# The first layer of whole expert tiles, computed turned from a standing copy of its weights

## The chip, the cores and the metric

The kernel runs on one core of one Trainium2 chip. The metric is device time in microseconds (us). Names of the engines: PE is the matrix engine (PEld its weight loads), DVE the vector engine, ACT the scalar engine, POOL and SP the two that mostly issue transfers here.

## What is computed

A graph layer of 4096 nodes with 512 features: masked attention over an adjacency matrix, then a mixture of experts. The change touches only the experts:

```
logits = xf @ Wg + bg                       # 8 experts
topk_scores, topk_idx = top_k(logits, 2)
topk_w = softmax(topk_scores)
h = gelu(einsum('nd,edh->neh', xf, W1) + b1)      # erf form
y = einsum('neh,ehf->nef', h, W2) + b2
out = sum over the 2 chosen experts of topk_w * y ; x = x + out
```

D = HID = 512, E = 8, everything in float32.

## The kernel before

The stages before the experts project q, k and v and build lists of neighbours (to about 456 us in the profile), run attention over gathered rows (to about 1455 us) and route the nodes (to about 1508 us): each node's normalized row is scattered into a buffer `xs_d` sorted by expert. The weights W1 and W2 of all 8 experts stand in SBUF from then on, in eight parts `wparts[c]` (parts 0 to 3 are the four 128-row chunks of W1, 4 to 7 those of W2), in the freed `ring` and one tile `w`.

The expert stage works through 66 tiles of 128 rows in an order written out by hand (`tiles`, L1464). 57 of them (`b < FULL`) hold rows of one expert: whole tiles. 9 are mixed (`b >= FULL`): their two halves of 64 rows belong to two experts, and the second half's weights are fetched for the tile into `wo_` by `load_other` (L1369, 8 transfers, and a ninth for its bias row `bo`). Mixed tiles stand in the sequence at place 7 and then every sixth.

The parts of one tile, each a function:

- `fetch` (L1287): SP loads the tile's rows.
- `turn` (L1362, L1364): PE transposes the rows in four pieces of 128x128 into `pt_e`, ACT copies them out as `xT`.
- `hidden` (L1393): loads the tile's expert number into registers of PE and DVE (L1395), and multiplies: four accumulating matmuls into `ph`, with a piece of `xT` standing in the array and 512 columns of W1 moving. DVE copies the result to `h` (L1407).
- `turn_hidden` (L1410): PE transposes `h` in four pieces into `pht`; DVE adds the bias `b1T` while it takes them out as `hT` (L1419), ACT applies gelu (L1424).
- `second` (L1427): four matmuls with a piece of `hT` standing and W2 moving, into `py`; DVE computes the row weights (L1438, L1441, L1444) and adds the bias row from `bb` (L1449; for the two halves of a mixed tile L1451 and L1452), ACT scales (L1453), and POOL scatters the rows into the output with an adding transfer (L1458).

Tiles overlap: in the loop of `tiles`, step n issues `turn_hidden(b)`, `hidden(after)`, `turn(third)`, `second(b)`, where `after` and `third` are the next two tiles; before a mixed tile `turn(third)` comes ahead of `hidden(after)`. Every engine executes its instructions in the order issued. Ahead of the first tile come 60 transposes that keep PE busy (`warm`, L1357) and `halves` (L1303 to L1349), in which DVE works out the table of the mixed tiles' experts, with two small matmuls (L1336) in its middle. A pool's tile with `bufs=1` is one buffer, so that its next writer waits for its last reader.

Of the kernel before, what the change touches and what calls it, by code (L numbers as in the profile page):

```python
# [9 lines left out]
F32 = mybir.dt.float32  # L10
# [10 lines left out]
P = 128  # L21
# [54 lines left out]
def _fast(ctx, tc, dram, flag, x, adj, Wks, Wqs, Wvs, Wo, Wg, bg, W1, b1, W2, b2, out):  # L76
    nc = tc.nc
    N, D = x.shape
    H, _, KD = Wks.shape
    E, _, HID = W1.shape  # L80
    DC = D // P
    HC = HID // P
# [17 lines left out]
    FULL = -(-(2 * N - E * (P - 1)) // P)  # L100
    Q = P // 2
# [232 lines left out]
    with ExitStack() as s1:  # L334
# [213 lines left out]
        for h in range(NHC):  # L548
# [4 lines left out]
            g, c = divmod(h, NH)  # L553
# [91 lines left out]
    with ExitStack() as s2:  # L645
# [81 lines left out]
        def turn(s):  # L727
            st = steps[s]
            i = st["i"]
            nk = len(st["kv"])  # L730
            pk = bank(f"pkT_{s}", [2 * NP, P])
            for x, g in enumerate(st["kv"]):
                for p in range(NP):
                    nc.tensor.transpose(pk[:, x * NP + p, :], g[:, ts(p, P)], ident)  # L734
            kT = step.tile([P, 2 * NP, P], F32, tag="kT", name=f"kT_{s}")
            nc.scalar.copy(kT[:, : nk * NP], pk[:, : nk * NP])  # L736
            st["kT"] = [kT[:, x * NP : (x + 1) * NP] for x in range(nk)]
            t = step.tile([P, NW, 16], U16, tag="t", bufs=6, name=f"t_{s}")
            if st["kind"] == "own":
                words = [own_words[:, i, :]]  # L740
            else:
                words = [wv[:, i * NW : (i + 1) * NW] for wv in st["wv"]]
            nw = NW // len(words)
            for x, wv in enumerate(words):
                w = slice(x * nw, (x + 1) * nw)
                nc.vector.tensor_tensor(
                    t[:, w], wv[:, w].unsqueeze(2).to_broadcast([P, nw, 16]), bits[:, w],
                    op=ALU.bitwise_and,
                )
            st["t"] = t.rearrange("p w k -> p (w k)")  # L750
            if st["kind"] == "own":
                m = step.tile([P, P], F32, tag="m", bufs=2, name=f"m_{s}")
                nc.vector.scalar_tensor_tensor(
                    m, st["t"], 0.0, eye, op0=ALU.is_gt, op1=ALU.max
                )
                st["m"] = m
# [507 lines left out]
    with ExitStack() as s4:  # L1264
# [89 lines left out]
        def warm():  # L1354
            pt = ps_t.tile([P, HC, P], F32, tag="t", name="pt_warm")
            for k in range(60):
                nc.tensor.transpose(pt[:, k % HC, :], ident, ident)  # L1357
# [11 lines left out]
        def load_other(b):  # L1369

            n = 2 * (b - FULL) + 1
            e = nc.values_load(
                tableq[:, n : n + 1], engines=(SP, DVE), min_val=0, max_val=E - 1,
                skip_runtime_bounds_check_because=why,
            )
            wo_ = otherp.tile([P, DC + HC, 1, HID], F32, tag="w", name=f"wo_{b}")
            for c in range(DC + HC):
                from_, k = (W1, c) if c < DC else (W2, c - DC)
                nc.sync.dma_start(
                    out=wo_[:, c],  # L1380
                    in_=from_[bass.ds(e, 1), ts(k, P), :].rearrange("e p f -> p e f"),
                )
            bo = otherp.tile([P, D], F32, tag="b", name=f"bo_{b}")
            nc.sync.dma_start(out=bo, in_=b2[bass.ds(e, 1), :].partition_broadcast(P))
            other[b] = e, wo_, bo

        def sides(b, c):
            w = wparts[c][:, bass.ds(es[b], 1), :]
# [1 line left out]
                return [(slice(0, P), w)]  # L1390
            return [(slice(0, Q), w), (slice(Q, P), other[b][1][:, c])]

        def hidden(b):  # L1393
            at = table[:, b : b + 1] if b < FULL else tableq[:, 2 * (b - FULL) :][:, :1]
            es[b] = nc.values_load(  # L1395
                at, engines=(PE, DVE), min_val=0, max_val=E - 1,
                skip_runtime_bounds_check_because=why,
            )
            ph = ps_h.tile([P, HID], F32, tag="h", name=f"ph_{b}")
            for c in range(DC):  # L1400
                for a, w in sides(b, c):
                    nc.tensor.matmul(  # L1402
                        ph[a], xTs[b][:, c, a], w, start=(c == 0), stop=(c == DC - 1),
                        skip_group_check=b >= FULL,
                    )
            h = work.tile([P, HID], F32, tag="h", name=f"h_{b}")
            nc.vector.tensor_copy(h, ph)  # L1407
            hs[b] = h

        def turn_hidden(b):  # L1410
            pt = ps_t.tile([P, HC, P], F32, tag="t", name=f"pht_{b}")
            for c in range(HC):
                nc.tensor.transpose(pt[:, c, :], hs[b][:, ts(c, P)], ident)
            hT = work.tile([P, HC, P], F32, tag="hT", name=f"hT_{b}")
            whose = [(slice(0, P), es[b])]
            if b >= FULL:
                whose = [(slice(0, Q), es[b]), (slice(Q, P), other[b][0])]
            for a, e in whose:
                nc.vector.tensor_tensor(  # L1419
                    hT[:, :, a], pt[:, :, a],  # L1420
                    b1T[:, bass.ds(e, 1), :].rearrange("p e c -> p (e c)").unsqueeze(2)
                    .to_broadcast([P, HC, a.stop - a.start]), op=ALU.add,
                )
            nc.scalar.activation(hT, hT, AF.Gelu)  # L1424
            hTs[b] = hT

        def second(b):  # L1427
            py = ps_y.tile([P, D], F32, tag="y", name=f"py_e{b}")
            for c in range(HC):
                for a, w in sides(b, DC + c):  # L1430
                    nc.tensor.matmul(  # L1431
                        py[a], hTs[b][:, c, a], w, start=(c == 0), stop=(c == HC - 1),
                        skip_group_check=b >= FULL,
                    )
            r = rows[b]
            wt = work.tile([P, 1], F32, tag="wt", name=f"wt_{b}")
            rest = work.tile([P, 1], F32, tag="rest", name=f"rest_{b}")
            nc.vector.tensor_scalar(  # L1438
                rest, r[:, D + 3 : D + 4], -1.0, 1.0, op0=ALU.mult, op1=ALU.add
            )  # L1440
            nc.vector.tensor_scalar(  # L1441
                wt, r[:, D + 1 : D + 2], pos[:, b : b + 1], rest, op0=ALU.is_equal, op1=ALU.mult,
            )
            nc.vector.tensor_scalar(  # L1444
                wt, wt, r[:, D + 3 : D + 4], r[:, D + 2 : D + 3], op0=ALU.add, op1=ALU.mult
            )
            y = work.tile([P, D], F32, tag="y", bufs=3, name=f"y_{b}")
            if b < FULL:
                nc.vector.tensor_add(y, py, bb[:, bass.ds(es[b], 1), :])  # L1449
            else:  # L1450
                nc.vector.tensor_add(y[:Q], py[:Q], bb[:Q, bass.ds(es[b], 1), :])  # L1451
                nc.vector.tensor_add(y[Q:], py[Q:], other[b][2][Q:])  # L1452
            nc.scalar.mul(y, y, wt)  # L1453

            n = P if b < FULL else Q
            for k in range(0, P, n):
                whose = r[:n, D : D + 1] if k == 0 else tokens[b]
                nc.gpsimd.indirect_dma_start(  # L1458
                    out=out,
                    out_offset=bass.IndirectOffsetOnAxis(ap=whose.bitcast(I32), axis=0),  # L1460
                    in_=y[k : k + n], in_offset=None, compute_op=ALU.add,
                )

        def tiles(seq, first=False):  # L1464
            mixed = [b for b in seq if b >= FULL]
            for b in seq[:4]:
                fetch(b)
            if first:
                nc.sync.dma_start(
                    out=bb.rearrange("p e f -> p (e f)"),  # L1470
                    in_=b2.rearrange("e f -> (e f)").partition_broadcast(P),
                )
                warm()
                halves()
            load_other(mixed.pop(0))
            turn(seq[0])
            hidden(seq[0])
            if len(seq) > 1:
                turn(seq[1])
            for n, b in enumerate(seq):  # L1480
                after, third = (seq[n + 1 : n + 3] + [None, None])[:2]
                if n + 4 < len(seq):
                    fetch(seq[n + 4])
                turn_hidden(b)
                if third is not None and after >= FULL:
                    turn(third)
                if after is not None:
                    hidden(after)
                if third is not None and after < FULL:
                    turn(third)  # L1490
                second(b)
                if b >= FULL and mixed:
                    load_other(mixed.pop(0))
# [565 lines left out]
```

## Time and profile before

| | us |
|---|---|
| timed runs, median of 3 (lowest, highest) | 2287.24 (2279.12, 2288.51) |
| profiled execution, its own time | 2042.98 |
| its span, first to last instruction | 2041.2 |
| busy in the span: PE, PEld | 1926.3, 1275.3 |
| busy: DVE, ACT, POOL | 968.6, 791.2, 569.4 |
| the expert stage in it | about 1508 to 2024, and a tail to the end |

The profile comes from one profiled execution. A line of it names the line of the kernel, the engine, the operation, what it writes and reads (`out<-in`), a count, busy time and mean length in ns. A matmul's record is longer than the time after which the next can start, since matmuls are pipelined: distances between starts are what counts. One float32 matmul has two records, for two passes, each with its own weight load; a transpose has one. The mean granted clock of PE was 0.981 of full speed.

### The profile page before, as it was taken

The numbers are of one execution on the slowest core, as the hardware profiler recorded it, in microseconds if no ns is written. First come the engines' busy times: TensorE is split into PE (matmuls) and PEld (weight loads), VectorE is DVE, ScalarE is ACT, GpSimd is POOL, SyncE is SP. The second block draws the span as 40 slices with busy tenths as digits, with TensorE's granted clock in tenths as the row PEclk, the third lists the DMA queues.
The fourth block names the chain that finished last, engine by engine and source line by source line (L and its number), as shares of the span: only waits on it lengthen the run. The fifth ranks groups of instructions, "written<-read, shape, count | busy, mean of one in ns | idle before, by whom it ended". The sixth has DMA issues, their size and how long they took to land. (4 is left out here: it accounts for less than half of the span.)

```text
span 2041.2 us, 59938 instructions
## 1 busy us (share of the span) xinstructions
PE 1926.3 (94%) x25581; PEld 1275.3 (62%) x25581; DVE 968.6 (47%) x2519; ACT 791.2 (39%) x1166; POOL 569.4 (28%) x716
## 2 busy tenths in 40 slices
PE   8799999998999898998999998999889999999997
PEld 4344444448887787887878887777654444444443
DVE  4455556634544464564555554454543333333332
ACT  3233333315555554654545454545312222222221
POOL 2000000016333326345362635324121222222221
PEclk9899999999999999999999999989989999999998
DMA  9877877249688859779687786858874555555542
GB/s 369 272 262 258 259 264 261 83 170 384 224 272 272 276 191 375 252 247 352 236 296 279 265 304 241 309 187 322 285 261 93 127 117 114 112 117 119 114 68 44
DMA packets 193602, 462.00 MB, mean 226 GB/s; under 512 B 30384, under 2 KB 46768, under 8 KB 193200
## 3 DMA queue, kind: packets, MB, share of 16 engines
q0 software_dynamic: 66784, 248.65, 38.4%
q1 hardware_dynamic: 102096, 178.04, 26.8%
q10 hardware_dynamic: 24448, 31.38, 4.5%
q8 instruction: 206, 3.38, 0.7%
q14 instruction: 68, 0.56, 0.1%
HBM read 385.37 MB, written 72.64 MB: 224 GB/s over the span
## 5 line engine op out<-in xcount | busy, mean ns | idle before, releaser
L707 POOL DMA_INDIRECT ring<-kv_d,idx x361 | 358.7, 994 | 851.7 <-issue 471.6
L778 ACT ACTIVATE pr<-ps 128x1024 f32<-128x1024 f32 x270 | 270.0, 1025 | 370.8 <-PE ps L771 367.0
L784 DVE SCALAR_TENSOR_TENSOR pr<-t,pr 128x1024 f32<-128x1024 uint16 x238 | 284.0, 1222 | 236.7 <-ACT pr L778 236.2
L771 PE MATMUL ps<-q,kT 64*64 64x64 f32 (+1 forms) x10224 | 306.6, 237 | 29.1 <-issue 23.8
L799 PE MATMUL o<-ring,pr 128*64 128x65 f32 x8640 | 297.3, 226 | 26.1 <-issue 26.0
L771 PEld LDWEIGHTS ps<-q,kT 64*64 64x64 f32 (+1 forms) x10224 | 273.0, 148 | 71.3 <-issue 55.1
L799 PEld LDWEIGHTS o<-ring,pr 128*64 128x64 f32 x8640 | 274.3, 140 | 54.0 <-issue 51.4
L1402 PE MATMUL ph<-ring,xT 128*128 (+1 forms) x528 | 238.2, 594 | 0.8 <-ACT xT L1364 0.8
L734 PE MATMUL pkT<-ident,ring 128*128 128x128 f32 x1572 | 209.6, 283 | 10.2 <-DMA ring<-kv_d 5.9
L736 ACT COPY kT<-pkT 128x512 f32<-128x512 f32 (+1 forms) x270 | 198.9, 786 | 15.9 <-PE pkT L734 10.3
L1458 POOL DMA_INDIRECT out_dram<-y,r x66 | 102.0, 1545 | 367.7 <-ACT y L1453 238.9
L734 PEld LDWEIGHTS pkT<-ident,ring 128*128 128x128 f32 x1572 | 173.6, 143 | 28.7 <-issue 8.9
L1431 PE MATMUL py_e<-ring,hT 128*128 (+1 forms) x396 | 182.3, 596 | 1.6 <-ACT hT L1424 1.6
L1402 PEld LDWEIGHTS ph<-ring,xT 128*128 128x128 f32 (+1 forms) x528 | 91.3, 183 | 99.8 <-issue 98.7
L1453 ACT ACTIVATE y<-y,wt 128x512 f32<-128x512 f32 x66 | 47.6, 722 | 269.8 <-DVE y L1449 230.0
L615 PE MATMUL pv<-wv,xT 128*128 128x512 f32 x256 | 130.0, 603 | 0.0
L1407 DVE COPY h<-ph 128x512 f32<-128x512 f32 x66 | 45.6, 691 | 170.7 <-PE ph L1402 170.7
L615 PE MATMUL pk<-wk,xT 128*128 128x512 f32 x256 | 125.2, 608 | 0.7 <-ACT xT L409 0.7
L600 PE MATMUL pq<-xT,wq 128*128 128x512 f32 x256 | 123.1, 603 | 0.0
L844 PE MATMUL py<-wo,oT 128*128 128x512 f32 x256 | 119.1, 609 | 0.7 <-ACT oT L838 0.7
L1073 POOL DMA_INDIRECT xs_d<-x,slot_i x58 | 67.8, 1169 | 173.4 <-DVE x L1069 58.5
L1431 PEld LDWEIGHTS py_e<-ring,hT 128*128 128x128 f32 (+1 forms) x396 | 67.2, 183 | 75.9 <-issue 74.1
(281 smaller groups left out, 1900.2 us busy)
## 6 DMA issues: line engine op xcount, KB each, us to landing
adj<-in_adj_dram SPq DMA_DIRECT2D x64, 1024.0 KB, 5.6
wo<-in_L_ffn_W_dram SPq DMA_DIRECT2D x72, 256.0 KB, 4.9
kv_d<-kvr ACTq DMA_DIRECT2D x32, 516.0 KB, 4.4
ring<-kv_d SPq DMA_DIRECT2D x32, 516.0 KB, 7.0
r<-xs_d SPq DMA_DIRECT2D x57, 258.0 KB, 2.7
ring<-in_L_ffn_W_dram SPq DMA_DIRECT2D x56, 256.0 KB, 3.3
xt<-in_x_dram SPq DMA_DIRECT2D x32, 256.0 KB, 6.9
q_d<-qT ACTq DMA_DIRECT2D x32, 256.0 KB, 4.3
```

Of the source, the lines that this page charges most:

```text
L600: nc.tensor.matmul(pq, w["q"][:, c, ts(p, P)], xTs[b][:, c, :], start=(c == 0), stop=(c == DC - 1),)
L615: nc.tensor.matmul(pk, xTs[b][:, c, ts(t, P)], w[n][:, c, :], start=(c == 0), stop=(c == DC - 1),)
L707: nc.gpsimd.indirect_dma_start(out=g, out_offset=None, in_=kv_d, in_offset=bass.IndirectOffsetOnAxis(ap=idx[i // GL][:, i % GL, a : a + 1] ...
L734: nc.tensor.transpose(pk[:, x * NP + p, :], g[:, ts(p, P)], ident)
L736: nc.scalar.copy(kT[:, : nk * NP], pk[:, : nk * NP])
L771: nc.tensor.matmul(ps[c : c + nk, r, p * P + x * nq : p * P + (x + 1) * nq], kT[r * KD : (r + 1) * KD, p, c : c + nk], q[r * KD : (r + 1) ...
L778: nc.scalar.activation(pr.rearrange("p h q -> p (h q)"), ps.rearrange("p r f -> p (r f)"), AF.Exp)
L784: nc.vector.scalar_tensor_tensor(pr, st["t"].unsqueeze(1).to_broadcast([P, H, P]), 0.0, pr, op0=ALU.is_gt, op1=ALU.mult,)
L799: nc.tensor.matmul(o[c * HALF : (c + 1) * HALF, h // NP, (h % NP) * VW : (h % NP + 1) * VW], pr[:, hd * NP + p, c * HALF : (c + 1) * HALF] ...
L844: nc.tensor.matmul(hold["py"], hold["oT"][:, c, :], wo[:, c, :], start=(c == 0), stop=(c == NP - 1),)
L1402: nc.tensor.matmul(ph[a], xTs[b][:, c, a], w, start=(c == 0), stop=(c == DC - 1), skip_group_check=b >= FULL,)
L1431: nc.tensor.matmul(py[a], hTs[b][:, c, a], w, start=(c == 0), stop=(c == HC - 1), skip_group_check=b >= FULL,)
```

## The change

For whole tiles the roles in the first layer are exchanged. A new function `stand` loads the expert number and lets DVE copy the expert's W1 (four pieces of 128x512, `w1s`, a single buffer) to a fixed place. `hidden` then has 128x128 pieces of `w1s` standing in the array and `xT` moving, in 16 matmuls of 128 columns into the four quarters of `ph`. The result comes out with hidden features on the partitions, as `second` wants it, so that the bias and gelu (now `gelu_`) follow at once from `ph`; the copy to `h` and the four transposes are issued for mixed tiles alone. `stand` is issued a tile ahead: after `hidden(after)` for `third`, and for the first tile ahead of `halves`. The bias row `bo` of a mixed tile's second half is no more fetched; it is read from `bb`. `h` has one buffer in place of two.

```diff
-            bo = otherp.tile([P, D], F32, tag="b", name=f"bo_{b}")
-            nc.sync.dma_start(out=bo, in_=b2[bass.ds(e, 1), :].partition_broadcast(P))
-            other[b] = e, wo_, bo
+            other[b] = e, wo_
...
-        def hidden(b):
+        w1s = {}
+        def stand(b):
             at = table[:, b : b + 1] if b < FULL else tableq[:, 2 * (b - FULL) :][:, :1]
             es[b] = nc.values_load(
                 at, engines=(PE, DVE), min_val=0, max_val=E - 1,
                 skip_runtime_bounds_check_because=why,
             )
+            if b < FULL:
+                w1s[b] = work.tile([P, DC, HID], F32, tag="w1s", bufs=1, name=f"w1s_{b}")
+                for c in range(DC):
+                    nc.vector.tensor_copy(
+                        w1s[b][:, c], wparts[c][:, bass.ds(es[b], 1), :].rearrange("p e f -> p (e f)")
+                    )
+
+        def hidden(b):
             ph = ps_h.tile([P, HID], F32, tag="h", name=f"ph_{b}")
+            if b < FULL:
+                pt = ph.rearrange("p (c t) -> p c t", t=P)
+                for f in range(HC):
+                    for c in range(DC):
+                        nc.tensor.matmul(
+                            pt[:, f, :], w1s[b][:, c, ts(f, P)], xTs[b][:, c, :],
+                            start=(c == 0), stop=(c == DC - 1),
+                        )
+                gelu_(b, pt)
+                return
...
-            h = work.tile([P, HID], F32, tag="h", name=f"h_{b}")
+            h = work.tile([P, HID], F32, tag="h", bufs=1, name=f"h_{b}")
...
         def turn_hidden(b):
+            if b < FULL:
+                return
             pt = ps_t.tile([P, HC, P], F32, tag="t", name=f"pht_{b}")
             for c in range(HC):
                 nc.tensor.transpose(pt[:, c, :], hs[b][:, ts(c, P)], ident)
+            gelu_(b, pt)
+
+        def gelu_(b, pt):
             hT = work.tile([P, HC, P], F32, tag="hT", name=f"hT_{b}")
...
-                nc.vector.tensor_add(y[Q:], py[Q:], other[b][2][Q:])
+                nc.vector.tensor_add(y[Q:], py[Q:], bb[Q:, bass.ds(other[b][0], 1), :])
...
                 warm()
+                stand(seq[0])
                 halves()
+            else:
+                stand(seq[0])
             load_other(mixed.pop(0))
             turn(seq[0])
             hidden(seq[0])
             if len(seq) > 1:
                 turn(seq[1])
+                stand(seq[1])
...
                 if after is not None:
                     hidden(after)
+                if third is not None:
+                    stand(third)
                 if third is not None and after < FULL:
                     turn(third)
                 second(b)
```

## The prediction

> **What bounds the kernel now.** The share of busy time by stage comes first, since the change touches only the last stage; its columns are the stretch in us, its length, then busy us (and records) of PE, PE's weight loads (PEld), DVE, ACT and POOL, the granted clock, DMA share and GB/s.
>
> ```profile
> 1455.00:1508.00 53.00, 40.63 (x333) 33.64 (x331) 31.14 (x182) 8.00 (x15) 17.04 (x32) 0.82 0.86 302
> 1508.00:2024.00 516.00, 513.84 (x1717) 243.10 (x1718) 177.65 (x413) 120.39 (x197) 112.10 (x74) 1.00 0.51 110
> 2024.00:2042.00 18.00, 3.56 (x8) 1.29 (x8) 0.69 (x1) 0.72 (x1) 2.68 (x2) 0.69 0.24 34
> ```
>
> For 516 us of expert tiles PE is busy 513.84 at full clock; DVE is busy a third of the time. A busy PE need not be a dense one, so the timeline of one whole tile follows (start, length, operation, count).
>
> ```profile
> 1583.22 0.60 PE L1413 MATMUL pht<-ident,h 128*128 128x128 f32 x4
> 1583.66 3.60 PE L1402 MATMUL ph<-ring,xT 128*128 x8
> 1587.10 0.60 PE L1362 MATMUL pt_e<-ident,r 128*128 128x128 f32 x4
> 1587.53 2.74 PE L1431 MATMUL py_e<-ring,hT 128*128 x6
> 1590.11 1.02 PE L1431 MATMUL py_e<-w,hT 128*128 x2
> 1590.97 0.49 PE L1413 MATMUL pht<-ident,h 128*128 128x128 f32 x3
> ```
>
> Starts follow without a hole: 4 transposes of the hidden result 0.44 us, first layer 3.44, 4 transposes of the input 0.43, second layer 3.44; 7.75 us a tile. One f32 matmul is two passes (8 records for 4 matmuls) and a pass of 512 columns takes 3.44 / 8 = 0.43. So PE's order of work is the path, and what leaves PE leaves the time. The waits confirm it: in the stage DVE waits for PE (h for ph, y for py_e), and PE waits for others only in the first and last tile.
>
> ```profile
> DVE h L1407 <- PE ph L1402: 170.7, 66, 4.3
> ...
> DVE y L1449 <- PE py_e L1431: 137.3, 57, 3.7
> ...
> PE py_e L1431 <- ACT hT L1424: 1.6, 1, 1.6
> ...
> PE pht L1413 <- DVE h L1407: 0.4, 1, 0.4
> ```
>
> (Total us, times, longest.)
>
> **Part 1: transposes removed.** 57 whole tiles lose turn_hidden's four, 0.44 us each tile on PE's path: 57 x 0.436 (a transpose starts every 0.109) = -24.9 us.
>
> **Part 2: the first layer turned.** Per whole tile, 4 matmuls with 512 moving columns become 16 with 128, so 8 passes become 32, each with its own 128-column weight load. Moving columns stay 8 x 512 = 32 x 128, so 3.43 us if loads hide. But a load must now hide behind a quarter of the streaming. How fast can load and pass follow each other? The trace has no f32 pass of 128 columns over the full array, but three neighbours:
>
> ```profile
> 489.56 1.75 PEld L771 LDWEIGHTS ps<-q,kT 64*128 64x128 f32 x29 [0.93 <-issue]
> ...
> 1479.23 0.97 PEld L954 LDWEIGHTS pl<-wg,x2T 128*128 128x128 f32 x8 [0.79 <-ACT x2T L924]
> ```
>
> The first has two-pass f32 matmuls, 128 weight columns and 128 moving columns, on half the rows, two halves side by side: (1.75 - 0.19) / 28 = 0.056 for a load, 0.111 in one half. The second has the full 128x128 weights but 8 moving columns: (0.97 - 0.19) / 7 = 0.111. (0.19 is one load's length, by the L771 and L954 rows.) The third is the transpose itself: full rows, 128 weight and 128 moving columns, 0.109. Here a rule of the Trainium skill speaks against the change: TensorE: Matmul & The Clock Gate, section "The mechanism" of Part 3, says that a weight load overlaps running matmuls only where its row group differs. All 32 loads here use all rows, so by the rule a pass would cost load plus stream, 0.107 + 0.107 = 0.214, and the layer 6.85 us instead of 3.43: the sum would be +170 us. (The same page's Part 2, "Step-by-step", allows a load ahead into a background buffer.) By the transposes' row, which uses all rows too and still keeps 0.109, the load hides. I go by the rows: 0.1115, so 32 x 0.1115 = 3.57 us, +0.14 a tile, 57 x 0.14 = +7.8 us. Bounds: 0.107 (nothing added; the streaming time excludes a gain) and 0.214. Parts 1 and 2 together: -17.1 us.
>
> **Part 3: the copies on DVE.** 228 copies (4 a tile) of 128x512 f32 from SBUF to SBUF, not in the trace. The row above is the copy out of PSUM, L1407, 692 ns; below, TENSOR_SCALARs within SBUF: 227 ns for 128x128 (L252) and 285 for 128x256 (L1247), so 58 ns for 128 elements more and 285 + 2 x 58 = 401 ns for 512. L392, 128x512 within SBUF, has a median of 546 with two per-row scalars, and such scalars cost 130 (L1441 273 against L1438 144): 416. I take 0.42, keep 0.69, and 4 x 0.42 = 1.7 us against the 0.69 removed: DVE's work a tile goes from 2.74 us (0.69 + 0.68 + 0.69 + 0.14 + 0.27 + 0.27) to 3.7 of 7.45, so it doesn't become the bound by volume.
>
> What matters is the hand-over. w1s has one buffer: copies for the next tile may start only when the first layer of the present one has been read, at T (its stream's end), and that next first layer needs them. Between lie turn (0.44) and second (3.43): T + 3.87. On DVE the bias add out of ph stands first (0.2 after T, as L1407 starts in the timeline, + 0.68), then a TENSOR_LOAD of the expert number by the sequencer (median 0.305, longest 0.92, beside the add, once that is issued), then the copies: T + 0.9 + 1.7 = T + 2.6. 0.1 us for a load of weights must still fit: 1.1 us to spare, so nothing is charged. With 0.69 for a copy it is T + 3.7: just covered. Behind the copies on DVE wait the three small wt operations (0.83 us, to T + 3.4) and y's add, which needs second's end (T + 4.07): covered. gelu on ACT needs only the add and comes a whole tile before second needs hT. ACT then copies xT at about T + 2.2, before T + 3.87.
>
> **Part 4: what else moves.** Value loads for PE and DVE move from hidden to stand; PE's (median 0.312, longest 0.97) run ahead in its sequencer, under a queued first layer of 3.5 us; if they didn't, 57 x 0.31 = 18 us would eat the gain. bo's 9 DMAs leave SP's queue, and y's lower half reads bb: same size of add (694 and 683 ns), nothing. SP and POOL are passed by nothing new. POOL's scatter (1.55 us) runs in the timeline from 1.9 us after second's end, inside the first layer, and is over before T: no meeting with the copies, except in 9 mixed tiles with two scatters. stand(0) now stands ahead of halves() on DVE: about 2.4 us (load and copies); the ring's weights were all issued by 1473 (L1159) and such loads land in 3.3 us by the page's median, so the copies needn't wait for them at 1497.5; halves' last operand was ready at 1501.25 while PE, in its 60 warming transposes, took it at 1505.8: covered by 4.5 us.
>
> Start: hidden(1) has only turn(1) ahead of it, so its copies show: T = 1508.14 + 3.57 = 1511.71, copies until 1514.1, start 1514.2, where it was 1513.21. +1.0 instead of this tile's -0.3: +1.3 us. End: from the last transposes' start (2021.63 in the timeline) to the last second layer's (2023.86) were 2.23 us; h is now turned long before, so these go, 0.44 of them counted already: -1.8 us.
>
> **Sum:** -17.1 + 1.3 - 1.8 = -17.6 us against the profiled execution's own 2042.98 (span 2041.2, 1.8 around it): 2025.4. The median of the timed runs is 2287.24, 1.12 times that; no view says which stage is longer there. The gain there is 17.6 if it is another stage, 19.7 if all stretch alike. I take 18.6: 2268.6 us. A measurement here can tell about 0.5%, 11.4 us, from no change.
>
> **Rivals.**
> Weights don't hide (slower): passes go at more than 0.121, where 32 passes eat the transposes' 0.44 as well. At 0.214 it is 57 x (6.85 - 3.87) = +170 us, 2457; at the load's own length of 0.19, +126, 2413. For it: the skill's rule, and no row has full rows, 128 moving columns and two passes at once. Against: each of the three rows has two of these and keeps 0.109 to 0.111.
> DVE hands over late (about the same to slower): PE waits for w1s after each second layer. It decides from copies ending after T + 3.8; each 0.1 us is 5.7 us. Slow copies (0.69) behind a slow value load (0.92): T + 0.3 + 0.92 + 2.76 = T + 4.0, 0.2 late, net -6 us, 2281; half a microsecond more[...]: +22, 2310. For: a single buffer, and L392's longest of 3.8 us shows that such an operation can stall. Against: 31 of its 32 didn't.
> The gain isn't there outside the profile: the timed runs' extra 244 us may be a limit of this stage that PE's work doesn't set, 2287. For: the unexplained gap. Against: nothing but PE is near its bound in the stage (DMA share 0.51). That the change doesn't do what it says is excluded by the order: 16 matmuls into ph, no transposes of it for whole tiles.
>
> **How the numbers follow.** Main case 0.68, 2259 (0.107 a pass, stretched) to 2276 (0.115 a pass, not stretched); weights 0.13; late hand-over 0.10, half of it within 0.5%, half slower; no gain 0.09. So faster 0.68, same 0.14, slower 0.18. The range runs from 2259 to 2298, into the late hand-over, and leaves out the weights' case.
>
> **What would show it.** Right: ph's matmuls of whole tiles 32 a tile, starting every 0.111; tile period 7.43; no pht but in 9 mixed tiles; COPY w1s near 0.42 and PE never waiting for w1s after the first tile. Wrong: PEld ph pitch near 0.2, or "PE ph <- DVE w1s" in the waits with tens of us, or DVE COPY w1s well over 0.7.

## The result: 17 us faster, and the profile after

| | before | after |
|---|---|---|
| timed runs of the comparison, median of 7 each (us) | 2279.12 (2273.47 to 2288.51) | 2261.99 (2247.55 to 2272.33) |
| profiled execution, its own time (us) | 2042.98 | 2247.55 |
| stretch: first `ph` matmul to start of last `py_e` matmul (us) | 1508.14 to 2026.96 = 518.83 | 1727.76 to 2228.95 = 501.18 |
| from that last `py_e` matmul to the end of the span (us) | 14.24 | 16.43 |

The ratio of the timed runs is 0.9925, with a 95% interval from 0.990 to 0.995: 17.1 us faster. The two profiled executions can't be subtracted: that of after is the longer by 200 us. Where those lie is seen first. This is the share of busy time by stage, of before and then of after; the columns are those of the same view in the prediction.

```profile
456.00:1455.00 999.00, 932.10 (x21054) 792.65 (x21056) 522.00 (x1202) 522.27 (x651) 417.77 (x483) 0.98 0.79 278
```

```profile
456.00:1672.00 1216.00, 1049.09 (x21062) 861.95 (x21064) 525.03 (x1203) 526.53 (x651) 411.15 (x483) 0.92 0.69 228
1672.00:1727.00 55.00, 39.46 (x327) 32.86 (x323) 31.46 (x180) 7.07 (x14) 16.88 (x32) 0.83 0.86 301
1727.00:2229.00 502.00, 499.75 (x2864) 341.32 (x2864) 221.27 (x587) 119.34 (x197) 113.78 (x74) 1.00 0.51 107
2229.00:2246.00 17.00, 0.54 (x2) 0.00 (x0) 0.69 (x1) 0.72 (x1) 1.99 (x2) 0.64 0.26 36
```

The attention stage, whose code is the same, took 1216 us instead of 999, with nearly the same number of PE records; transfers moved 228 GB/s instead of 278. The stages before and behind it are alike in length. So the kernels are compared by the stretch, which both executions ran at a granted clock of 1.00. It became 17.65 us shorter. What PE does in it is in the timeline of one whole tile of after (start, length, operation, count).

```profile
1801.61 3.73 PE L1413 MATMUL ph<-xT,w1s 128*128 128x128 f32 x32
1805.18 0.60 PE L1362 MATMUL pt_e<-ident,r 128*128 128x128 f32 x4
1805.61 2.74 PE L1455 MATMUL py_e<-ring,hT 128*128 x6
1808.19 1.02 PE L1455 MATMUL py_e<-w,hT 128*128 x2
1809.05 0.72 PE L1413 MATMUL ph<-xT,w1s 128*128 128x128 f32 x5
```

From start to start: first layer 3.57 us, turning the input 0.43, second layer 3.44; a tile starts every 7.44 us instead of 7.745. The transposes `pht` are gone, and 32 passes of 128 columns take 3.57 / 32 = 0.112 us each. DVE's part of the same tile:

```profile
1805.45 0.69 DVE L1443 TENSOR_TENSOR hT<-ph,b1T 128x512 f32<-128x512 f32 x1 [2.95 <-PE ph L1413]
1806.06 1.42 DVE L1403 COPY w1s<-ring 128x512 f32 x4
1807.40 0.14 DVE L1462 TENSOR_SCALAR rest<-r 128x1 f32<-128x1 f32 x1
```

With T = 1805.18, the end of the first layer's stream, the copies run from T + 0.88 to T + 2.30, and the layer that needs them starts at T + 3.87. In the costliest groups (count, busy us, mean ns, and idle time ahead with what ended it) stands what PE waited for:

```profile
L1413 PE MATMUL ph<-xT,w1s 128*128 128x128 f32 x1824 | 214.0, 276 | 2.3 <-ACT xT L1364 2.3
L1413 PEld LDWEIGHTS ph<-xT,w1s 128*128 128x128 f32 x1824 | 211.0, 192 | 27.8 <-issue 25.0 <-ACT xT L1364 2.8
L1403 DVE COPY w1s<-ring 128x512 f32 x228 | 82.0, 421 | 8.9 <-issue 7.1 <-DMA xs_d<-xn,slot_i 1.7
```

In 1824 passes PE was idle for 2.3 us, and no wait is put down to `w1s`. All 2.3 us belong to the first two tiles, and the engine named is ACT.

### The profile page after: what moved, and what is told of

The parts are those of the page before. It is cut to its first block, busy times and chain, and to the rows that moved or that the text cites. A ratio compares the mean times of both kernels' runs of the same rounds, so it can differ in the third digit from the quotient of the medians.

```text
span 2245.4 us, 62381 instructions
## 1 busy us (share of the span) xinstructions
PE 2027.1 (90%) x26721; PEld 1441.5 (64%) x26721; DVE 1015.1 (45%) x2690; ACT 793.3 (35%) x1166; POOL 563.4 (25%) x716
## 5 line engine op out<-in xcount | busy, mean ns | idle before, releaser
L707 POOL DMA_INDIRECT ring<-kv_d,idx x361 | 354.2, 981 | 1076.2 <-issue 471.6
L771 PE MATMUL ps<-q,kT 64*64 64x64 f32 (+1 forms) x10224 | 394.3, 246 | 102.7 <-issue 89.5
L771 PEld LDWEIGHTS ps<-q,kT 64*64 64x64 f32 (+1 forms) x10224 | 325.3, 153 | 180.1 <-issue 157.7
L799 PE MATMUL o<-ring,pr 128*64 128x65 f32 x8640 | 308.4, 227 | 37.3 <-issue 37.3
L799 PEld LDWEIGHTS o<-ring,pr 128*64 128x64 f32 x8640 | 281.2, 141 | 70.1 <-issue 67.0
L734 PE MATMUL pkT<-ident,ring 128*128 128x128 f32 x1572 | 222.8, 291 | 24.0 <-ACT pr L778 12.0
L1413 PEld LDWEIGHTS ph<-xT,w1s 128*128 128x128 f32 x1824 | 211.0, 192 | 27.8 <-issue 25.0
L1413 PE MATMUL ph<-xT,w1s 128*128 128x128 f32 x1824 | 214.0, 276 | 2.3 <-ACT xT L1364 2.3
L734 PEld LDWEIGHTS pkT<-ident,ring 128*128 128x128 f32 x1572 | 181.7, 148 | 47.3 <-issue 18.2
L1443 DVE TENSOR_TENSOR hT<-ph,b1T 128x512 f32<-128x512 f32 x57 | 39.4, 692 | 162.6 <-PE ph L1413 159.7
```

The source lines that it names most:

```text
L707: nc.gpsimd.indirect_dma_start(out=g, out_offset=None, in_=kv_d, in_offset=bass.IndirectOffsetOnAxis(ap=idx[i // GL][:, i % GL, a : a + 1] ...
L771: nc.tensor.matmul(ps[c : c + nk, r, p * P + x * nq : p * P + (x + 1) * nq], kT[r * KD : (r + 1) * KD, p, c : c + nk], q[r * KD : (r + 1) ...
L799: nc.tensor.matmul(o[c * HALF : (c + 1) * HALF, h // NP, (h % NP) * VW : (h % NP + 1) * VW], pr[:, hd * NP + p, c * HALF : (c + 1) * HALF] ...
L1413: nc.tensor.matmul(pt[:, f, :], w1s[b][:, c, ts(f, P)], xTs[b][:, c, :], start=(c == 0), stop=(c == DC - 1),)
```

## The experiments

Every number of a stretch is measured as above. The variants start from before or from after, as the diff shows.

**The scale: `before_again`.** The kernel before, without an edit, on a chip where the whole run takes 250 us longer than in its first profile. It asks whether the expert stage stretches with the rest.

> The kernel before once more. The stretch compared in all these runs goes from the first matmul of the first layer (ph) to the last one of the second layer (py_e) of the expert stage: 518.8 us in the profile of before, 501.2 after. Theory A (the gain is only a matter of PE's order in the expert stage, and the longer timed runs are longer elsewhere): 518.8 +- 0.3 us, whatever the whole span is, and any extra length lies in the attention stage. Theory B (the timed runs stretch all stages alike): 518.8 x (span / 2041.2).

Measured: span 2293.1 us, stretch 518.81. The expert stage doesn't stretch; the extra time lies in the attention stage, which took 1250 us here (456 to 1706) and not 999. A gain made here is the same number of microseconds in a short and in a long execution.

**Part 1 alone: `no_transposes`.** From after, without `stand`'s copies and with the first layer as in before. It leaves out the turning of the hidden result, so its output is that of another computation.

```diff
-            if b < FULL:
-                w1s[b] = work.tile([P, DC, HID], F32, tag="w1s", bufs=1, name=f"w1s_{b}")
...
-                            pt[:, f, :], w1s[b][:, c, ts(f, P)], xTs[b][:, c, :],
...
+                for c in range(DC):
+                    for a, w in sides(b, c):
+                        nc.tensor.matmul(ph, xTs[b][:, c, :], w, start=(c == 0), stop=(c == DC - 1))
```

> Part 1 alone: whole tiles keep the first layer of before (xT standing, 512 moving columns, no copies of weights), but h's copy and its transposes are left out and bias and gelu are taken straight from ph, so the hidden result stays unturned for whole tiles. Theory A: the stretch loses 57 x 0.436 = 24.9 us, the wait of 0.57 at the first tile and 1.8 at the end: 518.8 - 27.3 = 491.6 us. Rival (another wait takes the transposes' place, as ACT's gelu or DVE's add): more than 495.

Measured: 493.40, 1.8 us more than expected; the tile period is 7.31, so the transposes are worth 0.435 a tile, as costed. Of the 1.8 us, 1.6 lies in the first two tiles: from the first to the third first layer it took 13.09 us where before took 12.92, and the expectation had taken off 0.87 for two tiles' transposes and 0.57 for a wait. The second tile waits there for something that the expectation had not seen. `fixed_w1` and the last pair below show what it is.

**Part 2 alone: `narrow128` and `narrow256`.** From before: the roles stay, but the 512 moving columns go in pieces of 128, so that 32 passes each load their own weights; or in pieces of 256.

```diff
-                        ph[a], xTs[b][:, c, a], w, start=(c == 0), stop=(c == DC - 1),
...
+            step_ = 128 if b < FULL else HID
+            for f in range(0, HID, step_):
...
+                            ph[a, f : f + step_], xTs[b][:, c, a],
+                            w if b >= FULL else w[:, :, f : f + step_],
+                            start=(c == 0), stop=(c == DC - 1),
```

> Part 2 alone, without exchanging roles: the kernel before, with the first layer of whole tiles in pieces of 128 moving columns (16 matmuls with 32 weight loads in place of 4 with 8), everything else as before. Theory A (a load hides behind the pass ahead, and a pass of 128 columns is held at about 0.112 us by its load): 32 x 0.1117 - 3.432 = 0.142 us more a tile, 57 x 0.142 = +8.1: 526.9 us. Rival (weight loads don't overlap passes in the same rows of the array): 0.214 a pass, +3.4 a tile: 713 us.

> The kernel before, with the first layer of whole tiles in pieces of 256 moving columns (8 matmuls, 16 weight loads). Theory A (a pass takes the longer of its load, 0.112, and its stream, 256 columns in 0.2145): nothing added, 518.8 us to 519.5. Rival (every further load costs about 5 ns, hidden or not): 57 x 8 x 0.005 = +2.3: 521.1. Rival (loads don't overlap): 16 x 0.107 - 8 x 0.107 more a tile, +49: 568.

One tile of `narrow128` in the timeline:

```profile
1831.63 2.74 PE L1435 MATMUL py_e<-ring,hT 128*128 x6
1834.21 1.02 PE L1435 MATMUL py_e<-w,hT 128*128 x2
1835.07 0.60 PE L1417 MATMUL pht<-ident,h 128*128 128x128 f32 x4
1835.51 3.74 PE L1404 MATMUL ph<-ring,xT 128*128 x32
```

Measured: 526.98, tile period 7.882: 0.137 more than before, against 0.142 expected. The price of the narrow passes is there without any copy on DVE. With `narrow256` it is 519.96 and 7.765: 0.02 for 8 further passes, 2.5 ns each, between the two expectations. So a pass of 256 columns costs hardly more than half of one of 512, while one of 128 costs 0.112 where a quarter of 0.429 is 0.107. The Trainium skill, TensorE: Matmul & The Clock Gate, Part 1, "Wait — 56ns, not 53.3ns?", gives a fixed cost of about 2.5 ns for every matmul at full clock. That is the 256-column result; at 128 columns it explains less than half: (7.882 - 7.745) / 24 = 5.7 ns for each further pass. What the rest is, no run here shows.

**Part 3 alone: `copies_only`.** From after: the copies are made, and the first layer reads them, but as the moving operand; turned roles and missing transposes are undone.

```diff
+            if b < FULL:
+                return [(slice(0, P), w1s[b][:, c] if c < DC else wparts[c][:, bass.ds(es[b], 1), :])]
...
-            if b < FULL:
-                return [(slice(0, P), w)]
...
-                gelu_(b, pt)
-                return
...
-            if b < FULL:
-                return
```

> Part 3 alone: the kernel after's copies of W1 on DVE (one buffer, same place in the order), but the first layer in the roles of before, with xT standing and the copy moving 512 columns wide; h's copy and the transposes are back. Theory A (the copies lie beside PE's work, apart from the first tile): 518.8 + 0.8 for the second tile's first layer, which waits for its copies: 519.6 us. Rival (the copies hold PE up in each tile): more than 525.

Measured: 521.71. From the third tile on every period is that of before (the sum from the third first layer to the last is 493.71 in both), so the copies cost nothing per tile. But the first two tiles took 15.80 instead of 12.92. In the share of busy time by stretch, the last three columns are the granted clock, the DMA share and GB/s:

```profile
1503.00:1505.00 2.00, 0.30 (x3) 0.10 (x1) 1.49 (x10) 0.00 (x0) 0.00 (x0) 1.00 0.93 289
1505.00:1507.00 2.00, 0.83 (x5) 0.62 (x6) 1.17 (x8) 0.59 (x1) 0.00 (x0) 0.74 1.12 427
1507.00:1512.00 5.00, 5.00 (x6) 1.98 (x7) 0.00 (x0) 0.00 (x0) 0.00 (x0) 0.50 0.96 385
```

The first layer started at 1506.80, at half clock: a pass of 512 columns took 0.853. PE had done its 60 warming transposes by 1503.1 and was nearly idle until then. The waits of DVE (total us, times, longest), just before, say why:

```profile
DVE w1s L1403 <- DMA xs_d<-blank: 4.5, 2, 4.2
```

The first copy started at 1498.80, 4.2 us after the operation ahead of it (1.0 of this is the load of the expert number), and `halves` with its two matmuls is queued behind the copies. The trace names a transfer of rows, and it was not W1 that DVE waited for: the last packet of the weights ended at 1484.25. The check that held DVE passed at 1498.66, and the semaphore of POOL's last scatter of rows into `xs_d`, issued at 1492.37, was complete at 1498.62. Why the copy has to wait for that scatter, no view says.

**No hand-over: `fixed_w1`.** From after, without copies; all whole tiles take expert 0's W1 as standing weights, so that it leaves out the choice of expert in the first layer.

```diff
-                for c in range(DC):
-                    nc.vector.tensor_copy(
...
-                            pt[:, f, :], w1s[b][:, c, ts(f, P)], xTs[b][:, c, :],
+                            pt[:, f, :], wparts[c][:, 0, ts(f, P)], xTs[b][:, c, :],
```

> The kernel after without the copies: whole tiles take the first layer's weights from expert 0's place, whatever their expert (the choice of expert in the first layer is left out), turned and without transposes as after. Theory A: only the second tile's wait for its copies goes, 501.2 - 0.7 = 500.5 us. Rival (copies or their waits cost in each tile): below 498.

Measured: 501.24, the same as after within 0.1, and the same 7.44 a tile. From the third first layer to the last it took 477.87 us in both. The steady hand-over really is free. But the expected 0.7 us at the start didn't come: without any copy the second tile waits just as long, and PE's waits have one row:

```profile
PE ph L1407 <- ACT xT L1364: 2.3, 2, 1.5
```

**How much room: `copies_x2` and `copies_x3`.** From after, with each piece of W1 copied two or three times.

```diff
-                for c in range(DC):
+                for c in 3 * list(range(DC)):
```

> The kernel after with each copy of weights issued twice (8 a tile). In the trace of after the first copy starts 0.88 us after the first layer's stream ends (T), one starts every 0.335, one lasts 0.417, and PE is ready for the next first layer at T + 3.87. Eight copies end at T + 3.64, and 0.05 for the signal and 0.11 for the load fit until T + 3.80. Theory A (single-buffer hand-over with 1.4 us to spare for four copies): only the second tile is later, 501.2 + 1.3 = 502.5 us. Rival (the hand-over has no such slack, each 0.1 us of DVE's work counts): 55 x 1.34 = +74, 575 us. Rival (no wait at all by then): 501.2.

> The kernel after with each copy of weights issued three times (12 a tile): the copies end at T + 4.98, the first layer can start at T + 5.14 in place of T + 3.87. Theory A: 1.27 us more in each of 55 tiles and 2.7 in the second: 501.2 + 72.5 = 574 us, and timed about 72 us slower than the kernel after, 55 slower than before (ratio 1.024). Rival (DVE's copies gate nothing as long as DVE is not full; it would be busy 6.4 of 7.4 us): 504.

Measured: `copies_x2` 503.72 with the same 7.44 a tile; all its loss is in the first two tiles, where the clock was 0.50 again. `copies_x3` gave 538.88, period 8.04: 0.60 more a tile and not 1.27. The whole time is 1.0137 of before (1.0091 to 1.0182). Its DVE, then its PE, in the same tile:

```profile
1598.38 0.69 DVE L1443 TENSOR_TENSOR hT<-ph,b1T 128x512 f32<-128x512 f32 x1 [2.04 <-PE ph L1413]
1598.99 4.11 DVE L1403 COPY w1s<-ring 128x512 f32 x12
```

```profile
1602.23 4.08 PE L1413 MATMUL ph<-xT,w1s 128*128 128x128 f32 x32
1606.15 0.60 PE L1362 MATMUL pt_e<-ident,r 128*128 128x128 f32 x4
```

Here T = 1598.11. The layer starts at T + 4.12, before the copies end at T + 4.99, and takes 3.92 to the next operation instead of 3.57: 0.25 lost ahead of it and 0.35 inside. Each matmul waits for its own piece. The fourth piece is wanted first by the seventh pass, 0.67 us into the layer, so the deadline for the last copy is about T + 3.87 + 0.67 = T + 4.5; by the 0.60 lost it is T + 4.99 - 0.60 = T + 4.4. The copies of after, ending at T + 2.30, have about 2.1 us to spare. (The 12 copies took 4.11 us, which is 11 x 0.335 + 0.42: a copy starts 0.335 us after the one ahead of it.)

**The start: `turn_first` and `fixed_w1_turn_first`.** From after and from `fixed_w1`: the second tile's input is turned ahead of the first tile's first layer.

```diff
             turn(seq[0])
-            hidden(seq[0])
             if len(seq) > 1:
                 turn(seq[1])
+            hidden(seq[0])
+            if len(seq) > 1:
                 stand(seq[1])
```

> The kernel after with one order changed: the second tile's input is turned (turn(seq[1])) ahead of the first tile's first layer instead of behind it, so that on ACT the copy xT of the second tile stands ahead of the gelu of the first. Theory A (the wait ahead of the second tile is ACT's: its xT copy stands behind gelu(0), which waits for DVE's add behind the first layer): xT is then there early, and only the copies of w1s are left. Each matmul waits for its own piece: in the kernel after, the fourth copy ended 1733.67, and the matmul that needs it is the seventh pass of the layer, due 6 x 0.112 = 0.67 us after the layer's start, so the layer starts as if at 1733.67 + 0.05 - 0.67 = 1733.05 instead of 1733.52: 0.47 us earlier, stretch from the first ph matmul to the last py_e matmul 500.7 instead of 501.2. Rival B (DVE's copies as a whole are the wait, as the prediction had it): nothing changes, 501.2. Rival C (neither counts): the layer follows without a gap, 499.1. In the whole time 0.5 us can't be seen: the same as the kernel after, about 17 to 18 us below before.

> The same order (second tile's input turned ahead of the first tile's first layer) in the variant that makes no copies and takes expert 0's W1 for every whole tile (so its result is that of other weights). Theory A (at the second tile ACT's xT copy behind gelu(0) was the only wait once the copies are gone): no wait is left; the gap of 2.25 us ahead of the second first layer, of which 0.11 is one pass, closes: stretch 501.24 - 2.14 = 499.1. Rival B (something else ahead of the second tile holds PE, such as the registers' value load or DVE's add): the stretch stays near 501.2. Later tiles keep 7.44 in both.

Measured: 500.72 and 499.00, each within 0.1 of theory A. (The stretch now begins behind the second tile's transposes. This hides nothing: from the first transpose `pt_e` to the first `ph` matmul it took 1.43 to 1.44 us in after, in `fixed_w1` and in both variants.) PE's waits in `turn_first` show the change of the releaser:

```profile
PE ph L1413 <- DVE w1s L1403: 1.2, 1, 1.2
...
PE ph L1413 <- ACT xT L1364: 0.4, 1, 0.4
```

So in after the second tile waits for ACT. ACT executes in order, gelu of the first tile stands ahead of the copy of the second tile's `xT`, and gelu waits for DVE's add behind the first layer. By the stretch, `turn_first` is the shortest kernel here that computes everything. Its timed median is 2262.55 us, 0.9936 of before (0.9916 to 0.9955): half a microsecond can't be seen there beside the 0.9925 of after.

**The clock at the start: `copies_x2_warm90` and `after_again`.** `copies_x2` with 90 warming transposes, and after once more on the same chip.

```diff
-            for k in range(60):
+            for k in range(90):
```

> copies_x2 (each piece of W1 copied twice) with 90 warming transposes in place of 60, that is 30 x 0.109 = 3.3 us more work for PE ahead of the expert stage. Question: why did the stage begin late by more than its copies in copies_x2 (first tile 5.33 us from its first layer's start to the turn, in place of 3.67) and in copies_only (6.49 in place of 3.54). Theory A (the first copies wait for W1's transfers, the halves' operand comes late, PE stands idle behind its warming transposes, and its granted clock is down to 0.50 when the first layer starts): with the longer warming PE is busy until that operand comes, the granted clock is 1.00 in the first layer, 3.67 us from its start to the turn, and the stretch from the first ph matmul to the last py_e matmul is 503.72 - 1.66 = 502.1. Rival B (the low clock has another cause, such as the copies themselves or the transfers at the same time): the first layer stays at 5.3 us and the stretch at 503.7.

> The kernel after, once more, on the same chip as copies_x2_warm90. Theory A (idle PE ahead of the first layer lowers the clock): what this run shows depends on when W1's transfers land. If the first copy of w1s starts over 2 us after DVE is ready for it, PE idles behind the warming transposes and the first tile takes up to 3 us more, stretch 503 to 504; if not, the first tile takes 3.67 us and the stretch is 501.2. Rival B (the low clock comes from something that only the variants have): 501.2 in both cases. Tile period 7.44 in the steady part in all.

Measured: 502.06 and 501.19. In `copies_x2_warm90` the clock holds:

```profile
1736.00:1740.00 4.00, 4.00 (x40) 3.99 (x39) 0.36 (x2) 0.00 (x0) 0.00 (x0) 1.00 0.97 402
1740.00:1741.00 1.00, 0.53 (x7) 0.29 (x4) 0.81 (x5) 0.31 (x1) 0.00 (x0) 1.00 0.42 180
1741.30:1745.00 3.70, 3.67 (x32) 3.67 (x33) 0.33 (x2) 0.00 (x0) 0.00 (x0) 1.00 0.79 271
```

Eight copies ran ahead of this, and transfers reach 402 GB/s, so neither is enough to lower the clock; PE was busy, and it stayed at 1.00. This agrees with A, but it is not a clean test of the longer warming: on this chip the first copy started 1.8 us after the operation ahead of it on DVE and not over 4 us after it, so that 60 transposes might have been enough. `after_again` had the same 1.8 us, and no idle PE. (A's first link, that the copies wait for W1's transfers, is not what happened; see `copies_only`.) All runs together say more: behind the warming transposes PE stood waiting for 1.4, 2.8 and 4.3 us in `copies_only`, `copies_x2` and `copies_x3`, and there alone the first layer ran at half clock, wholly or for the most part; in the other eleven profiles it had no such wait, and the clock was 1.00.

## Why the prediction was right, point by point

The predicted time was 2268.6 us; 2262 was measured, and the change of 17.1 us stands beside the sum of 17.6.

- *What bounds the kernel.* Right: what left PE's stream left the time. PE is busy 499.75 of 502 us after the change too.
- *Part 1, -0.436 a tile.* Right: -0.435 in `no_transposes`.
- *Part 2, +0.14 a tile by a pass of 0.1115.* Right: 0.112, and +0.137 alone in `narrow128`. The rule weighed against it (a load overlaps only where its row group differs) is refuted here: 1824 loads with all rows, 192 ns each by their records, follow each other every 112 ns with the passes. Load and pass one behind the other, 0.213 apart, stand only 11 times: between the first and second pass of the first two tiles, which had just waited, and of the nine layers that follow a mixed tile's second layer, where PE had not waited. Not everything is hidden: 0.112 is above the 0.107 of the streaming alone, and `narrow256` shows that 2.5 ns come with each further pass of 256 columns too; that the rest is the load isn't shown.
- *Part 3, hand-over charged nothing.* Right, and with more room than worked out. Copies ended at T + 2.30 (T + 2.6 predicted), since a record of 0.419 us overlaps the next and they start every 0.335. The step "it decides from copies ending after T + 3.8" was too strict: `copies_x3` puts the point near T + 4.4, since matmuls wait piece by piece.
- *Part 4, nothing else moves.* Not shown wrong for after in two profiles. The step "the copies needn't wait for them at 1497.5" holds for W1's transfers, whose last packet had ended 10 us or more before DVE came to them. But the 2.4 us for load and copies were too few: the first copy started 1.7 us after the operation ahead of it in after and 4.2 in `copies_only`, and the last ended 3.6 and 6.2 after it. In after this was hardly a wait: the load took until 1718.20, then checks of semaphores followed, about 0.1 us each, until 1719.21. In `copies_only` one of these checks waited 2.3 us for the last scatter into `xs_d`, which the prediction did not ask about. The cover of 4.5 us by the warming transposes shrank to 1.4 in after (last operand of `halves` written at 1724.92, taken at 1726.28) and to nothing in `copies_only`, where idle PE then lost its clock.
- *Start, +1.3.* The size was near, the reason wrong. From the first tile's first layer to the third's it took 13.30 us instead of 12.92: +0.38, where +1.3, less the 0.3 that Parts 1 and 2 count for each of the two tiles, makes +0.7. The wait was said to be for `w1s`; it is for ACT's `xT`. With ACT ready, the copies still held the layer, only 0.47 us less (`turn_first`), so the two waits nearly coincide, and it is by luck that the size came out near.
- *End, -1.8.* Right on PE and lost behind it. From the last first layer to the last second layer it took 10.01 us instead of 12.20: -2.19, the 1.8 and the transposes counted already. But the tail grew by 2.19 (16.43 against 14.24). POOL's last two scatters, of before and of after, by the timeline:

```profile
2023.56 1.56 POOL L1458 DMA_INDIRECT out_dram<-y,r  x1 [5.75 <-ACT y L1453]
2029.32 1.56 POOL L1458 DMA_INDIRECT out_dram<-y,r  x1 [4.20 <-ACTq L1505]
```

```profile
2227.87 1.56 POOL L1482 DMA_INDIRECT out_dram<-y,r  x1 [5.45 <-ACT y L1477]
2233.41 1.56 POOL L1482 DMA_INDIRECT out_dram<-y,r  x1 [3.98 <-issue]
```

In before the last rows were ready at 2029.04 and scattered 0.28 later. In after they were ready at 2231.08, but the scatter came 2.33 later: 5.54 after the one ahead of it. In all nine profiles that end as after does, the last rows were ready 3.5 us behind the rows ahead of them, and their scatter came 5.2 to 5.8 us behind the scatter ahead. Behind mixed tiles, where POOL has a scatter more to catch up with, the next ones come 5.5 to 5.7 apart in after, so that a scatter of a whole tile seems to hold POOL's queue for about 5.5 us; the trace names no releaser, so this is inferred. POOL is what is late next, and the prediction did not ask. (The tail was 14.2 to 15.5 in before, `before_again`, `narrow128` and `narrow256`, and 16.0 to 17.0 in all kernels that end as after does. In `copies_only`, which ends as before does, it was 16.1. There and in the two narrow variants the last scatter came 1.2 to 1.4 us after its rows, 6.7 to 6.8 behind the one ahead, and not 0.3 as in before; this stays unexplained.) So from the first `ph` matmul to the end of the span it was 533.06 before and 517.62 after: -15.4, not -17.6 (533.67 and 517.73 in `before_again` and `after_again`). The timed -17.1, with an interval from -23 to -11, can't tell these apart. That the stretch lost 17.65 where the sum says 17.6 is partly luck: the start was less dear than predicted, the steady tiles gave a little less, and the tail is not in it.

- *The scale.* Choosing 18.6 between 17.6 and 19.7 was needless. `before_again` shows that the expert stage doesn't stretch, so 17.6 was the number to carry over.
- *The rivals.* Weights that don't hide: refuted by 0.112. Late hand-over: refuted by `fixed_w1`, which has none and is no faster. Copies slowed by POOL: not seen; 30 of the 228 ran beside the record of a scatter, with a median of 0.418 us, and the others with 0.419. Gain not there outside the profile: refuted by the timed runs.

## What to carry to other kernels

Where PE's stream is the bound, an operation removed from it is worth its pitch, read from starts in the timeline, and a copy on another engine that prepares its operands is free as long as it ends before the pass that first reads its piece. Check both ends of the pipeline by hand, though, with every in-order queue in them: at the start ACT's order decided, not the copies that the change brought, and at the end POOL's scatters took back what PE gave. Anything put on an engine ahead of the first tile can also be paid twice, as a delay and then as a slower clock: in `copies_only` the first layer started 12.1 us after the first warming transpose and not 10.5, and the first two tiles then took 2.9 us longer.

## What was not expected of the hardware

- The granted clock of PE. In `copies_only` it was 1.00 until 1505.94, 2.8 us after the warming transposes had ended, and then 0.50 for 6.83 us, with PE busy in 6.0 of them. In `copies_x2` it fell 2.3 us after the transposes, for 6.83 us, and in `copies_x3` 2.05 us after them, for 10.24: twice and three times 3.41. The Trainium skill, TensorE: Matmul & The Clock Gate, Part 1, "The HAM clock gate", has a gate that halves the clock after a window of about 3.4 us of idleness and restores it after as long a busy one, the windows running free. The lengths agree with such windows, and so does the return, at the end of the first one that PE filled. The fall came sooner than the page would have it: in each of the three, PE was still at its transposes for some part of the 3.41 us ahead of it, in `copies_x3` for 1.4 of them. The first layer of before, with only four transposes in the 2.1 us ahead of it, ran at full clock.
- The attention stage with the same code took 999 us in one execution and 1216 and 1250 in others, and the runs of one chip lay all near the one or all near the other. In the long one fewer bytes a second were moved. Why stays open.
- A copy of 128x512 f32 within SBUF is 419 ns long by its record, and the next starts 335 ns after its start.
